# Order of the last routing steps and of the first expert chunks' loads in a gated cross-attention and mixture-of-experts kernel

## The chip, the core and the metric

The kernel runs on one core of one Trainium2 chip. The metric is the device time of one execution in microseconds (us). Runs of the kernel before took 369.24 to 371.98 us, with a median of 370.11 us over three runs.

## The reference

Cut to what matters:

```python
x = x + tanh(g_x) * attention(layernorm(x), ctx, ctx)       # 16 heads of 64, causal
def ffn(x):                                                  # 8 experts, 128 -> 512 -> 128
    e = argmax(softmax(x @ Wr + br))                         # one expert for each token
    out = 0
    for i in range(8):
        xi = x * (e == i)                                    # zero row for other tokens
        out = out + relu(xi @ W1[i] + b1[i]) @ W2[i] + b2[i]
    return out
x = x + tanh(g_f) * ffn(layernorm(x))                        # x: 8 x 256 x 128
```

There are 2048 tokens. A token whose expert is not i still gets `relu(b1[i]) @ W2[i] + b2[i]` from expert i. The kernel adds those constants up beforehand, so that every token is worked on by its own expert alone.

## The kernel before

**Attention.** The eight sequences are taken in four pairs, and each pair in eight steps of two heads: 32 steps, numbered g. A step makes queries, keys, values, scores, exponentials, transposed probabilities and products. A pair's output, its second layer norm and its routing run beside the next pair's steps. The last pair has no next one, so its rest is written out by hand in `last_turns` and `last_routing`. There it is split into two halves, one for each sequence: `a` and `b`, both of class `Half`.

**A half.** `residual` and `out(c)` add the residual and the eight head pairs' share of the output projection into the PSUM tile `y`. `attend` makes the last steps' values in the PSUM tile `o` and evicts them to SBUF, on DVE (L724) or ACT (L726). `statistics` copies `y` to `rows` on ACT (L730), takes the statistics on DVE (L735, L737) and makes the standard deviation on POOL (L739, L740). `turned`, `logits`, `normalized` and `choice` pick each token's expert (`hot`). `apply` writes the normalized rows on ACT (L777). `places` counts on PE (L648 to L652) and on DVE (L653 to L658) at which row of its expert's region of the DRAM array `store` each token goes. `scatter` sends 128 rows there by an indirect DMA from POOL (L673).

**Chunks.** An expert's tokens are worked on in chunks of 128 rows of `store`. There are 23 chunks: `NA` = 5 early ones, which are full before the last pair's tokens come; 8 own ones, one for each expert, whose weights stand ready in SBUF; and 10 later ones, called "rest". Which rows a chunk loads is computed on the device: `plan_full` for the early and own chunks, `plan_rest` for the later ones, 18 short DVE instructions (L846). SyncE (SP) reads a chunk's number (`fetch_number`, L867), asks for its 132 KB of rows (`fetch_rows`, L871) and, for an early or a later chunk, for its expert's 578 KB of weights from the DRAM copy `later` (`fetch_weights`, L881). All of these go through one SP queue in the order of the code.

**A chunk's work.** `turned_rows` transposes the rows (PE L903) and copies them (DVE L905). `first_layer` is eight matmul records on PE (L912), `hidden` four activations on ACT (L920), `residual_rows` adds the constants (L886, on POOL or DVE), `second_layer` is eight matmul records on PE (L928), `sums` adds up (DVE L939), and `store_out` scatters to the output (POOL L946). `second_layer` writes one of two PSUM buffers named `misc`, which it gets back when the `sums` two chunks before has read it.

**Order.** The whole kernel stands under a manual schedule: every engine works off its instructions in the order of the code. In `last_routing`, the early chunks' layers are interleaved with half `b`'s routing. `experts` then loads and works on the own and the later chunks. The rows of own chunks come from `store`, so SP asks for the first of them only when the scatters of the last half have landed. In the text below, r0 to r4 are the rows and w0 to w4 the weights of the early chunks 0 to 4, and r5 are the rows of the first own chunk.

Of the kernel before, what the change touches and what calls it, by code (L numbers as in the profile page):

```python
# [18 lines left out]
B, S, D = 8, 256, 128  # L19
# [16 lines left out]
NA = 5  # L36
# [12 lines left out]
def tile_gated_xattn_moe(  # L49
# [17 lines left out]
    banks = [ps_s.tile([P, 2, 512], F32, tag=f"sc{b}", name=f"sc_{b}") for b in range(2)]  # L67

    def misc(name):
        return ps_m.tile([P, 512], F32, tag="misc", name=name)  # L70
# [197 lines left out]
    _, first = counted("first", [E], [[N, E]])  # L268
# [265 lines left out]
    def turn(g, i):  # L534

        b, j = i // 2, i % 2
        pr = prob[g, b]
        ps = ps_t.tile([P, 512], F32, tag="pt", name=f"pt_{g}_{i}")
        for n in range(3):
            nc.tensor.transpose(ps[:, n * P : (n + 1) * P], pr[:, j, K0 + n * P : K0 + (n + 1) * P], ident)  # L540
        pt = p5.tile([P, 3 * P], F32, tag="probT", name=f"probT_{g}_{i}")
        nc.vector.tensor_copy(pt, ps[:, 0 : 3 * P])  # L542
        probT[g, i] = pt
        if j == 1:
            prob.pop((g, b))
# [125 lines left out]
    def scatter(n, place=None):  # L671
        p, t = n // 4, n % 4
        ins = nc.gpsimd.indirect_dma_start(  # L673
            out=store,
            out_offset=bass.IndirectOffsetOnAxis(ap=places[p][:, t : t + 1] if place is None else place, axis=0),
            in_=rows[:, n],
            in_offset=None,
            bounds_check=E * N - 1,
            oob_is_err=True,
        )  # L680
        free_order(ins, "store")
        if p == NPAIR - 1:
            tc.declare_no_dep(ins.ins, group="full", reason="full chunks have no row left for the last pair's tokens")


    class Half:
# [41 lines left out]
        def statistics(self):  # L728

            nc.scalar.activation(  # L730
                self.rows[:, :, D : 2 * D], self.y.rearrange("p (t d) -> p t d", d=D), AF.Identity
            )
            st, mv = self.tile("st", 2, 6), self.tile("mv", 2, 2)
            for i in range(2):
                nc.vector.bn_stats(st[:, i], self.y[:, i * D : (i + 1) * D])  # L735
            for i in range(2):
                nc.vector.bn_aggr(mv[:, i], st[:, i])  # L737
            self.mv, ve, self.dev = mv, self.tile("ve", 2), self.tile("dev", 2)
            nc.gpsimd.tensor_scalar(ve, mv[:, :, 1], EPS, None, ALU.add)  # L739
            nc.gpsimd.tensor_tensor(self.dev, ve, half, ALU.pow)  # L740

# [40 lines left out]
        def places(self, start, end):  # L782
            places[NPAIR - 1, self.h] = places_of(f"last{self.h}", self.hot, self.n, self.sum, self.pos, start, end, 2)

        def scatter(self):
            for i in range(2):
                scatter(4 * (NPAIR - 1) + self.ts[i], places[NPAIR - 1, self.h][:, i : i + 1])
                apart()

# [53 lines left out]

    def plan_rest():

        q = lambda f, *args: f(*args)  # L846
        n = const.tile([P, E], F32, name="n_rest")
        q(nc.vector.tensor_tensor, n, cb[NPAIR], first, ALU.subtract)
        q(nc.vector.scalar_tensor_tensor, n, done, -float(P), n, ALU.mult, ALU.add)
        m = full_chunks(q, "rest", n, ALU.is_gt, NDYN)  # L850
        whose, k, _ = owners(q, "rest", m, NDYN, done)
        q(nc.vector.tensor_scalar, k, k, 1.0, None, ALU.add)
        q(nc.vector.scalar_tensor_tensor, k, whose, float(NT), k, ALU.mult, ALU.add)
        chunk_of["rest"] = const.tile([P, NDYN], I32, name="load_rest")
        q(nc.vector.tensor_copy, chunk_of["rest"], k)

    chunk_of = {}
    chunks = store.rearrange("(c p) r -> c p r", p=P)
# [16 lines left out]
    def fetch_weights(i):  # L875
        if NA <= i < NA + E:
            w = ws[:, i - NA]
        else:
            at = (W_FULL + i if i < NA else (i - NA - E) % NW) * WROW
            w = arena[:, at : at + WROW]  # L880
            nc.sync.dma_start(out=w, in_=later[bass.ds(number[i] // NT, 1)].rearrange("o p r -> (o p) r"))  # L881
        weights[i] = w[:, 0:FF], w[:, FF:WROW]

    def residual_rows(i, engine):
        r, v = loaded[i], weights[i][1]
        engine.tensor_tensor(r[:, D : 2 * D], r[:, D : 2 * D], v[:, AT_C : AT_C + D], ALU.add)  # L886
# [6 lines left out]
    def turned_rows(ids, beside=False):  # L893

        if not beside:
            ps = h_of[ids[0]] = hidden_bank(ids[0])
            ps = ps[:, 1]
        else:
            ps = ps_t.tile([P, 512], F32, tag="pt", name=f"xs_{ids[0]}")
        n = len(ids)  # L900
        t = p2.tile([P, 512], F32, tag="kT", name=f"xsT_{ids[0]}")
        for k, i in enumerate(ids):
            nc.tensor.transpose(ps[:, k * P : (k + 1) * P], loaded[i][:, 0:D], ident)  # L903
            xsT[i] = t[:, k * P : (k + 1) * P]
        nc.vector.tensor_copy(t[:, 0 : n * P], ps[:, 0 : n * P])  # L905

    def first_layer(i):
        w, x = weights[i][0], xsT.pop(i)
        if i not in h_of:
            h_of[i] = hidden_bank(i)  # L910
        for c in range(NHC):
            nc.tensor.matmul(  # L912
                h_of[i][:, 0, c * P : (c + 1) * P], lhsT=w[:, c * P : (c + 1) * P], rhs=x, start=True, stop=True
            )

    def hidden(i):
        ps, v = h_of.pop(i), weights[i][1]
        h = hT[i] = p2.tile([P, NHC, P], F32, tag="qT", name=f"h_{i}")
        for c in range(NHC):
            nc.scalar.activation(  # L920
                h[:, c], ps[:, 0, c * P : (c + 1) * P], AF.Relu, bias=v[:, AT_B1 + c : AT_B1 + c + 1]
            )
# [37 lines left out]
        nc.gpsimd.memset(warm[:, 0:1], 0.0)  # L960

    def fetch_full():
        for i in range(NA):
            fetch_number(i)
            fetch_rows(i)
        for i in range(NA):
            fetch_weights(i)

    def last_turns():


        g, l = NG - 2, NG - 1
        a = Half(0, misc("y_last0")[:, 0:S], misc("o_last0")[:, 0:S], banks[1][:, 0])
        b = Half(1, banks[0][:, 1, 0:S], banks[0][:, 0, 0:S], banks[1][:, 1])
        steps = plan_full()

        def plan(n):
            for _ in range(min(n, len(steps))):
                f, *args = steps.pop(0)
                f(*args)  # L980

        scatter(8)
        normalized(l, 0)
        turn(g, 0)
        turn(g, 1)
        exps(l, 1)
        scatter(9)
        normalized(l, 1)
        for n in (10, 11):
            scatter(n)  # L990
            apart()
        a.residual()
        a.out(*range(NC - 3))
        plan(4)
        turn(l, 0)
        turn(l, 1)
        a.attend(g, nc.scalar)
        plan(5)
        a.out(NC - 3)
        turn(g, 2)  # L1000
        turn(g, 3)
        a.attend(l, nc.scalar)
        plan(len(steps))
        fetch_full()
        a.out(NC - 2)
        b.residual()
        b.out(0)
        a.out(NC - 1)
        a.statistics()
        turn(l, 2)  # L1010
        turn(l, 3)
        a.turned()
        b.out(1, 2)
        a.logits()
        b.attend(g, nc.vector)
        a.normalized()
        a.choice()
        b.out(3)
        b.attend(l, nc.scalar)
        a.apply()  # L1020
        a.places(cb[NPAIR - 2], cb[NPAIR - 1])
        a.scatter()
        b.out(4, 5, 6, 7)
        return a, b

    def last_routing(a, b):


        e = range(NA)
        b.statistics()  # L1030
        turned_rows(e[:2], True)
        b.turned()
        turned_rows(e[2:], True)
        b.logits()
        b.normalized()
        b.choice()
        first_layer(e[0])
        b.apply()
        hidden(e[0])
        b.places(cb[NPAIR - 1], cb[NPAIR])  # L1040
        first_layer(e[1])
        hidden(e[1])
        second_layer(e[0])
        for i in e[:2]:
            residual_rows(i, nc.gpsimd)
        nc.gpsimd.tensor_copy(early_ids, rows[:, 0:NA, 2 * D : 2 * D + 1].rearrange("p i o -> p (i o)").bitcast(I32))
        b.scatter()
        for i in e[2:]:
            residual_rows(i, nc.gpsimd)
        sums(e[0])  # L1050
        first_layer(e[2])
        hidden(e[2])
        second_layer(e[1])
        sums(e[1])
        plan_rest()
        for i in e[3:]:
            first_layer(i)
            hidden(i)
            second_layer(i - 1)
            sums(i - 1)  # L1060
        second_layer(e[-1])
        sums(e[-1])

    def experts():
        own, more = range(NA, NA + E), range(NA + E, NCH)
# [212 lines left out]
```

## Time and profile before

| what | us |
|---|---|
| median of three runs | 370.11 |
| lowest, highest | 369.24, 371.98 |
| the profiled execution | 369.71 |
| its span, first to last instruction | 367.9 |
| PE busy in the span | 344.5 (94%) |
| DVE, POOL, ACT busy | 240.9, 214.4, 207.5 |
| mean granted TensorE clock | 0.984 |

The profile shows one execution on one core. A row of the timeline gives the start, the busy time, the engine, the source line, the operation with its tiles, and in brackets the idle time just before it with what ended it. The chain of waits starts from the last instruction and goes back, at each step to what released it. A window's row gives its length, the busy time of each engine and the granted clock of TensorE (PEclk, 1.00 is full speed). PE stands for matmuls, PEld for their weight loads, SPq for SyncE's queue of DMA issues. A matmul's end is modelled, so neighbouring records overlap.

### The profile page before, as it was taken

How to read it: one execution, taken by the hardware profiler on the slowest of the kernel's cores; microseconds unless marked ns; L12 is line 12 of the kernel's file. 1: busy time of each engine (PE TensorE's matmuls, PEld its weight loads, DVE VectorE, ACT ScalarE, POOL GpSimd, SP SyncE). 2: the span in 40 equal slices, each digit the busy share in tenths (PEclk: the TensorE clock that was granted, in tenths of full speed). 3: DMA queues.
4: the chain of work that ended last, by engine and by line, in shares of the span. 5: the costliest groups of instructions: out<-in, count | busy, mean ns of one | idle time of the engine just before them, and what ended most of it. 6: DMA issues, size and time to landing. Idle time of an engine off the chain costs nothing.

```text
span 367.9 us, 7926 instructions
## 1 busy us (share of the span) xinstructions
PE 344.5 (94%) x2598; PEld 247.7 (67%) x2598; DVE 240.9 (65%) x838; ACT 207.5 (56%) x743; POOL 214.4 (58%) x306
## 2 busy tenths in 40 slices
PE   8979999999999999999999899999999895979993
PEld 3335666567677776667776566677666774969993
DVE  3637777675667677886766877846788885254441
ACT  2466687755555758555575485555666513436551
POOL 4136665671555577769773388683666663407673
PEclk9899999999999999999999999999999999699999
DMA  6999777766599992000000000075000016679910
GB/s 202 288 164 186 111 114 118 191 240 181 181 385 384 385 384 108 2 2 2 3 0 16 15 16 16 2 321 211 16 16 18 15 61 205 238 215 344 407 50 13
DMA packets 36319, 53.57 MB, mean 146 GB/s; under 512 B 3801, under 2 KB 22829, under 8 KB 36280
## 3 DMA queue, kind: packets, MB, share of 16 engines
q1 hardware_dynamic: 28280, 44.07, 35.0%
q0 software_dynamic: 7360, 8.73, 12.4%
q8 instruction: 20, 0.33, 0.4%
q10 hardware_dynamic: 640, 0.29, 0.3%
q14 instruction: 19, 0.16, 0.1%
HBM read 27.82 MB, written 25.71 MB: 146 GB/s over the span
## 4 chain that ended last, share of the span: by engine, by line
PE 71%; DVE 9%; ACT 9%; DMA 4%; issue 3%; POOL 1%; POOLq 0%; SPq 0%; DVEq 0%; ACTq 0%
PE sc L478 11%; PE o L553 10%; PE pt L540 9%; PE q L438 7%; ACT prob L509 6%; PE y L592 6%; PE k L445 6%; PE v L456 5%; PE hs L912 4%; PE ys L928 4%; DMA arena<-later 3%; DVE sc L488 3%; PE sc L467 2%; ACT kT L447 2%; PE y_last L710 1%
## 5 line engine op out<-in xcount | busy, mean ns | idle before, releaser
L509 ACT ACTIVATE prob<-sc,nmax 128x129 f32<-128x129 f32 (+1 forms) x256 | 105.1, 425 | 92.3 <-DVE nmax L488 92.3
L532 POOL TENSOR_TENSOR prob<-prob,rs 128x256 f32<-128x256 f32 (+1 forms) x128 | 102.6, 858 | 64.8 <-DVE rs L523 64.7
L540 PEld LDWEIGHTS pt<-ident,prob 128*128 128x128 f32 x384 | 46.8, 141 | 52.8 <-issue 47.5
L542 DVE COPY probT<-pt 128x384 f32<-128x384 f32 x128 | 67.1, 544 | 14.8 <-PE pt L540 14.7
L540 PE MATMUL pt<-ident,prob 128*128 128x128 f32 x384 | 63.8, 278 | 1.7 <-DVE probT L542 1.7
L488 DVE CUSTOM_DVE_ANT_0 sc<-sc,bias 128x256 f32<-128x256 f32 x128 | 55.3, 432 | 4.4
L509 ACT ACTIVATION_READ_ACCUMULATOR prob<-sc,nmax 128x1 f32 x256 | 53.5, 209 | 0.0
L478 PE MATMUL sc<-kT,qT 64*128 64x128 f32 (+1 forms) x512 | 50.6, 337 | 0.0
L553 PE MATMUL o<-probT,v 128*64 128x256 f32 x480 | 45.6, 332 | 0.0
L553 PEld LDWEIGHTS o<-probT,v 128*64 128x64 f32 x480 | 29.7, 136 | 18.3 <-issue 8.0
L478 PEld LDWEIGHTS sc<-kT,qT 64*128 64x128 f32 x512 | 36.3, 187 | 4.9
L486 DVE TENSOR_REDUCE nmax<-sc 128x2 f32<-128x258 f32 x64 | 27.0, 421 | 14.7 <-PE sc L478 14.5
L438 PE MATMUL q<-xT,arena 128*128 128x512 f32 x64 | 34.0, 613 | 1.5 <-DVE xT L410 0.8
L445 PE MATMUL k<-cT,arena 128*128 128x512 f32 x64 | 34.4, 620 | 0.8 <-DVE total L336 0.8
L456 PE MATMUL v<-arena,cT 128*128 128x512 f32 x64 | 33.1, 600 | 1.5 <-ACT qT L440 1.5
L440 ACT ACTIVATE qT<-q,bqT 128x512 f32<-128x512 f32 x32 | 22.0, 688 | 13.2 <-PE q L438 12.5
L523 DVE RECIPROCAL rs<-ssum 128x4 f32<-128x4 f32 x64 | 11.0, 173 | 27.7 <-ACT prob L509 22.9
L946 POOL DMA_INDIRECT out_dram<-o,rows x18 | 17.9, 992 | 18.9 <-DVE o L939 15.1
L920 ACT ACTIVATE h<-hs,arena 128x128 f32<-128x128 f32 x60 | 17.1, 367 | 14.3 <-ACT h L920 8.9
L447 ACT ACTIVATE kT<-k,bT 128x512 f32<-128x512 f32 x32 | 22.2, 693 | 3.7 <-PE k L445 3.7
L569 DVE TENSOR_SCALAR arena<-o,bT 128x512 f32<-128x512 f32 x30 | 22.4, 746 | 1.2 <-PE o L553 1.2
L592 PE MATMUL y<-wo_sb,arena 128*128 128x128 f32 x192 | 23.1, 275 | 0.0
(243 smaller groups left out, 505.0 us busy)
## 6 DMA issues: line engine op xcount, KB each, us to landing
store<-blank SPq DMA_DIRECT2D x16, 1056.0 KB, 14.7
arena<-later SPq DMA_DIRECT2D x15, 578.0 KB
rows<-in_ctx_dram POOLq DMA_DIRECT2D x5, 1024.0 KB, 9.1
later<-ws SPq DMA_DIRECT2D x1, 4624.0 KB
rows<-store SPq DMA_DIRECT2D x23, 132.0 KB, 3.7
ws<-in_L_ffn_W_dram SPq DMA_DIRECT2D x1, 2048.0 KB
ws<-in_L_ffn_W_dram SPq DMA_DIRECT2D x8, 256.0 KB, 6.6
x<-in_x_dram SPq DMA_DIRECT2D x4, 256.0 KB
```

The costliest lines, as they stand in the source:

```text
L438: nc.tensor.matmul(ps, lhsT=wq_sb[:, c * P : (c + 1) * P], rhs=xT[p], start=True, stop=True)
L445: nc.tensor.matmul(ps, lhsT=wk_sb[:, c * P : (c + 1) * P], rhs=cT[p], start=True, stop=True)
L447: nc.scalar.activation(kT[g], ps, AF.Identity, bias=bT[:, NC + c : NC + c + 1])
L456: nc.tensor.matmul(ps, lhsT=cT[p][:, t * P : (t + 1) * P], rhs=wv_sb[:, c * P : c * P + 512], start=True, stop=True)
L478: nc.tensor.matmul(s[:, j, at : at + n], lhsT=q[r, b * S + t * P : b * S + (t + 1) * P], rhs=k[r, b * S : b * S + n], start=(t == 1), stop ...
L488: nc.vector.tensor_tensor_reduce(out=s[:, j, K1:U1], in0=s[:, j, K1:U1], in1=bias[:, 2 * (g // NC) + b, K1:U1], scale=-1.0, scalar=-NEG_AL ...
L509: nc.scalar.activation(pr[:, j, lo:hi], s[:, j, lo:hi], AF.Exp, bias=m[:, t, j : j + 1], scale=-1.0 if t else 1.0, accum_out=sm[:, t, j : ...
L532: nc.gpsimd.tensor_tensor(pr[:, :, lo:hi], pr[:, :, lo:hi], r, ALU.mult)
L540: nc.tensor.transpose(ps[:, n * P : (n + 1) * P], pr[:, j, K0 + n * P : K0 + (n + 1) * P], ident)
L542: nc.vector.tensor_copy(pt, ps[:, 0 : 3 * P])
L553: nc.tensor.matmul(o[DK * j : DK * (j + 1), n * P : S], lhsT=v[:, 2 * b + n, cols], rhs=probT[g, 2 * b + j][:, 0:S] if n == 0 else probT[g ...
L592: nc.tensor.matmul(ps[:, i * D : (i + 1) * D], lhsT=attT[p * NC + c][:, t * P : (t + 1) * P], rhs=wo_sb[:, c], start=(c == 0), stop=(c == ...
```

## The change

- `fetch_full` asks for the early chunks' weights between their rows. The order at SP was r0, r1, r2, r3, r4, w0, w1, w2, w3, w4; it becomes r0, r1, w0, r2, r3, w1, r4, w2, w3, w4.
- In `last_turns`, `a.o` moves from a `misc` buffer to the first half of `banks[0]`, `b.o` from the first to the second half of `banks[0]`, and `b.y` from that second half to a `misc` buffer. Four of `b.out`'s last eight matmuls come ahead of `a.places`; `a`'s second scatter moves into `last_routing`.
- `statistics` is cut in two: `deviation` holds its two POOL instructions. For `b`, `deviation` stands ahead of `a`'s second scatter.
- In `last_routing`, `b.turned`, `b.logits` and the first layer and the hidden activations of chunk 0 come ahead of the transposes of chunks 2 to 4. `b.apply` follows chunk 0's activations. The first layer of chunk 1 comes ahead of `b.places`, its activations follow. `b`'s scatters come ahead of the copy of `early_ids`.
- `plan_rest` gives back its 18 instructions as a list. They are issued five at a time between the sums of the early chunks, where they were all issued after the sums of chunk 1.

```diff
@@ class Half
-            self.mv, ve, self.dev = mv, self.tile("ve", 2), self.tile("dev", 2)
+            self.mv = mv
+
+        def deviation(self):
+            mv, ve, self.dev = self.mv, self.tile("ve", 2), self.tile("dev", 2)
             nc.gpsimd.tensor_scalar(ve, mv[:, :, 1], EPS, None, ALU.add)
             nc.gpsimd.tensor_tensor(self.dev, ve, half, ALU.pow)
...
-        def scatter(self):
-            for i in range(2):
+        def scatter(self, *which):
+            for i in which:
@@ def plan_rest
-        q = lambda f, *args: f(*args)
+        steps = []
+        q = lambda *step: steps.append(step)
...
+        return steps
@@ def fetch_full
+        weights_behind = {1: (0,), 3: (1,), 4: (2, 3, 4)}
         for i in range(NA):
             fetch_number(i)
             fetch_rows(i)
-        for i in range(NA):
-            fetch_weights(i)
+            for k in weights_behind.get(i, ()):
+                fetch_weights(k)
@@ def last_turns
-        a = Half(0, misc("y_last0")[:, 0:S], misc("o_last0")[:, 0:S], banks[1][:, 0])
-        b = Half(1, banks[0][:, 1, 0:S], banks[0][:, 0, 0:S], banks[1][:, 1])
+        a = Half(0, misc("y_last0")[:, 0:S], banks[0][:, 0, 0:S], banks[1][:, 0])
+        b = Half(1, misc("y_last1")[:, 0:S], banks[0][:, 1, 0:S], banks[1][:, 1])
...
         a.statistics()
+        a.deviation()
...
         a.apply()
+        b.out(4, 5)
         a.places(cb[NPAIR - 2], cb[NPAIR - 1])
-        a.scatter()
-        b.out(4, 5, 6, 7)
+        a.scatter(0)
+        b.out(6, 7)
@@ def last_routing
         e = range(NA)
+        steps = []
+        plan = lambda n: [f(*args) for f, *args in [steps.pop(0) for _ in range(min(n, len(steps)))]]
         b.statistics()
+        b.deviation()
+        a.scatter(1)
         turned_rows(e[:2], True)
         b.turned()
-        turned_rows(e[2:], True)
         b.logits()
         b.normalized()
         b.choice()
         first_layer(e[0])
+        hidden(e[0])
+        turned_rows(e[2:], True)
         b.apply()
-        hidden(e[0])
+        first_layer(e[1])
         b.places(cb[NPAIR - 1], cb[NPAIR])
-        first_layer(e[1])
         hidden(e[1])
         second_layer(e[0])
         for i in e[:2]:
             residual_rows(i, nc.gpsimd)
+        b.scatter(0, 1)
         nc.gpsimd.tensor_copy(early_ids, rows[:, 0:NA, 2 * D : 2 * D + 1].rearrange("p i o -> p (i o)").bitcast(I32))
-        b.scatter()
         for i in e[2:]:
             residual_rows(i, nc.gpsimd)
+        steps += plan_rest()
         sums(e[0])
-        first_layer(e[2])
-        hidden(e[2])
-        second_layer(e[1])
-        sums(e[1])
-        plan_rest()
-        for i in e[3:]:
+        for i in e[2:]:
             first_layer(i)
             hidden(i)
+            plan(5)
             second_layer(i - 1)
             sums(i - 1)
+        plan(5)
         second_layer(e[-1])
         sums(e[-1])
+        plan(len(steps))
```

## The prediction

> **What bounds the kernel now.** I read the page first (PE busy 94% of the span), then the chain of waits over the end, then the timeline of the stretch in which the chain leaves PE, then windows for the clock.
>
> ```profile
> PE 344.5 (94%) x2598; PEld 247.7 (67%) x2598; DVE 240.9 (65%) x838; ACT 207.5 (56%) x743; POOL 214.4 (58%) x306
> 306.82 2.12 DMA rows<-store
> 309.95 10.07 DMA arena<-later
> 320.10 0.35 DVE o L939
> 320.45 0.12 DVE n_rest L846
> ...
> 324.32 0.06 DVE load_rest L846
> 324.44 0.36 DVE o L939
> ```
>
> The number ahead of each piece of the chain is its start. PE holds the chain until 305 and again from 326.77. Between, it passes through a load of rows, 10 us of weights and 4 us of the plan's DVE instructions. The timeline of that stretch has the steps that I shall move:
>
> ```profile
> 303.17 0.71 PE L710 MATMUL sc<-wo_sb,arena 128*128 128x128 f32 x4 [0.59 <-DVE arena L724]
> 305.26 2.05 PE L710 MATMUL sc<-wo_sb,arena 128*128 128x128 f32 x16 [0.32 <-ACT arena L726]
> 312.22 2.05 PE L912 MATMUL hs<-xsT,arena 128*128 128x128 f32 x8 [2.56 <-DMA arena<-later]
> 317.42 0.98 POOL L673 DMA_INDIRECT store<-rows,posi_last  x1 [0.18 <-ACT h L920]
> 321.01 6.02 SPq L871 DMA_DIRECT2D rows<-store  x9
> 324.94 1.13 PE L928 MATMUL ys<-arena,h 128*128 128x128 f32 x8 [1.37 <-DVE o L939]
> 326.77 1.16 PE L912 MATMUL hs<-xsT,ws 128*128 128x128 f32 x8 [0.59 <-DVE xsT L905]
> ```
>
> The reader sees PE wait 2.56 us for w0, the last half's second scatter at 317.42, r5 asked for only at 321.01 (the SP waits name that scatter, 5.6 us), a PE wait behind the plan, and the first own chunk's first layer at 326.77. From there PE is busy 34.52 of 35.60 us, one chunk each 1.89 us, to the end at 367.9. So the time is **326.77 plus a fixed 41.1 us of span, plus 1.8 us around it** (369.71 against 367.9). What moves the start of that layer moves the end. My sum stands against 369.71, which lies 0.4 below the median of 370.11, inside the runs' spread.
>
> ```profile
> 7.70:11.10 3.40, 1.97 (x10) 1.15 (x10) 1.86 (x5) 1.65 (x4) 1.66 (x9) 1.00 0.75 207
> 11.10:14.50 3.40, 3.40 (x4) 1.39 (x5) 3.40 (x15) 0.69 (x1) 0.00 (x0) 0.50 1.10 346
> 284.20:287.60 3.40, 1.95 (x31) 1.53 (x29) 3.13 (x11) 2.85 (x14) 1.37 (x2) 1.00 0.00 0
> 308.10:311.50 3.40, 1.01 (x9) 0.69 (x6) 2.46 (x13) 1.26 (x3) 1.86 (x4) 1.00 0.97 307
> 311.50:318.30 6.80, 6.08 (x32) 6.04 (x33) 1.14 (x7) 2.28 (x8) 3.13 (x6) 0.50 0.92 354
> ```
>
> In these windows the second figure is PE's busy time and the last but two the granted clock. After 1.01 us of PE work in 3.40, the clock is at half for 6.8 us: eight matmul records take 2.05 us there instead of 1.06.
>
> **The change, part by part.**
>
> *PSUM tiles.* `b.out(3)` at 303.17 reads a head pair that was long in SBUF, yet waits for the DVE eviction of `b.o`, and `b.out(4)` at 305.26 for the ACT one: `b.y` and `b.o` are halves of one tile, `banks[0]`. With `b.y` in `misc` both waits go. `b.out(3)` (0.45) runs under the DVE eviction, `b.attend` starts at 303.17 instead of 303.81, `b.out(4, 5)` (0.89) fills the wait for `hot`, `a.places` takes 0.3, `b.out(6, 7)` 0.89: `b.y` is done at about 306.1 instead of 307.3. `a.places` is some 0.4 later by it, and `a`'s first scatter starts at 307.0 instead of 306.58; nobody waits for that one alone. `a.o` in `banks[0]` costs nothing: the exponentials that read it ended at 291.9, its first matmul was at 294.69.
>
> *`deviation` ahead of `a`'s second scatter.* On POOL the first scatter (1.08, memset 0.12) ends at 308.1 and the statistics are there by 307.4, so `dev` comes at 309.2, where it was 310.04; the choice follows in 1.6 (310.08 to 311.68), so `hot` is there at 310.85. Queued behind `dev` is `a`'s second scatter, 307.96 before, 309.4 now. In this stretch a scatter has taken up to 7.4 us to land (the rows' tile view: 2.1/3.3/7.4), so 316.8 at worst, still ahead of `b`'s.
>
> *Loads on SP.* A weight issue takes 0.58 to 0.65 of SP, a number with its rows 1.17. r0 and r1 stay at 301.44 and 303.18; w0 goes out at 303.83 (307.47 before), r2 and r3 at 305.1 and 306.3, w1 at 306.9 (308.04), **r4 at 308.1 (306.82)**, then w2 to w4 at 308.7 to 309.9, as before. w0 landed 4.65 after its issue (307.47 to 312.12), w1 and the others some 2.0 apart (314.0 ... 320.0). So w0 lands near 308.0 (3.3 to 4.65 after its issue: 307.1 to 308.5), and w4 near 317.3, since one of five loads of 2 us each is out of the way early, or 320.0 if the cadence doesn't hold. r4 is what this part costs. Alone, rows land 2.1 after their issue; now 578 KB stand ahead. The trace has one queue serving r4 and then w0, w1 ... in order. The Trainium skill, "DMA: Bandwidth & Descriptors" (Queues, rings and completion order), speaks against the change here: each DMA engine consumes a ring in ring order, so small rows can't pass large weights. By the 2.1 us of the rows alone r4 would land at 310.2; by the rule it lands behind w1, 306.9 + 3.3 to 4.65, plus 0.6 of its own: 310.8 to 312.2. I take 311.4, since the cadence of 2.0 is nearer to the short end and `a`'s scatter shares the engines.
>
> *Order on PE.* Logits end at about 308.0; the first layer of chunk 0 (0.89 at full clock) runs 308.0 to 308.9, against 312.22 to 314.24. Then the transposes of chunks 2 to 4 wait for r4: 311.4 to 311.75, and behind them stand chunk 1's first layer (to 312.7) and `b.places` (to 313.0; before 314.3). `hot` (310.85) is no longer what is late; r4 is. ACT has chunk 0's activations (1.14) and then `b.apply` (0.88) done by 311.1, ahead of any use.
>
> *The scatter and r5.* From the end of `b.places` to the first scatter it was 1.7 (314.3 to 316.02), to the second 1.4 more, from there to SP's release 3.4 (320.82), to the issue 0.2, to landing 2.1, to the first layer of chunk 5 about 0.8 (transpose, copy). From 313.0 that gives 314.7, 316.1, 319.5, 319.7, 321.8, **322.6**. Behind the scatters stand `early_ids` (0.2) and the residuals of chunks 2 to 4 (0.45 each) on POOL: chunk 2's sum waits for its own until about 317.9, and its buffer is wanted by chunk 4's second layer at 319.5.
>
> *The plan in steps.* 18 instructions took 320.37 to 324.49, 0.23 each. Five are 1.15, with a sum 1.5, beside 1.79 of PE for two layers: hidden. The PE wait of 1.37 and the late copy of chunk 5 go. Were r5 in no better time than before (asked at 321.01, landed 323.1), this part alone would be worth 1.5. Chunk 4's layers follow w4: 317.3, first layer 318.3, activations 1.14, second layer to 320.4, so PE is free before r5 lands.
>
> **Sum.** 326.77 - 322.6 = 4.2 earlier: 369.71 - 4.2 = **365.5 us**. The bounds: r4 at 310.8 and a scatter that lands in 2.4 (317.42 to 319.8, if the last straggler is another DMA's doing) give 321.0, held by PE to about 321.2: 364.1. r4 at 312.2 gives 323.4: 366.3.
>
> **Rivals.**
>
> *The clock drops all the same (0.27).* PE now idles from 308.9 to 311.4, 2.5 us, much as the 2.56 before, but between two first layers. The skill, "TensorE: Matmul & The Clock Gate" (Why this matters for your kernels), asks for gaps under some 3 us; by it neither gap should have cost a thing. The windows above say otherwise: 1.01 us of work in 3.40 was followed by half clock, and so was 1.97 at 7.70, nearly all transposes, while 1.95 of mixed work at 284.20 was not. So the kind of work counts beside the gap, and the new window has 0.7 to 1.3 us, with matmuls in it. By the rule 365.5. By the row, six groups of eight at half clock add 1.0 each, partly under the weights' arrival: the second layer of chunk 4 ends at 323.8, chunk 5 starts at 324.6: **367.5**. I take full clock, since the quiet window before had only transposes and logits.
>
> *Rows behind weights (0.06, the other side).* Chunks 2 to 4's transposes stand ahead of chunk 1 and of `b.places` on PE. If the engines mix r4 with w1 to w4 instead of serving them in order, r4 lands with the last, near 317.5, and everything from `b.places` on moves 6.1: 328.7, **371.6**. It decides once r4 lands after 315.6. For it: `a`'s scatter took 7.4 us in this traffic. Against: w0 and w1 landed one by one.
>
> *Given back later (0.05).* The later chunks' weights become the end: **369.7**. The last of them was issued at 345.89, needs some 3.4, and is used at 326.77 + 17 x 1.89 = 358.9: 9.6 us of room against 4.2 taken. So it is unlikely.
>
> **Chances.** Forecast 0.62, the rivals as given. Both of the first are below 369.7, so 363.9 to 368.4 holds eight in ten. A change of 1%, about what a measurement of this kernel tells from none, is 366.4: the forecast's case lies below it nine times in ten, the half-clock case seldom. Faster 0.60, within 1% 0.36, slower 0.04.
>
> **What would show it.** Right: L710 of `b.out` without a wait for L724 or L726; a first layer at about 308.0; PE's wait for rows until 311 to 312 at L903; the second scatter near 316; no wait of L928 for L939; chunk 5's first layer at 322 to 323. Wrong: a granted clock of 0.50 after 311; r4 landing past 313; chunks at the end further apart than 1.89.

## The result and the profile after

The kernel after took **367.36 us** (median of ten runs, 365.03 to 369.84) against 370.24 us for the kernel before beside it: a ratio of 0.9916, with a 95% interval from 0.9892 to 0.994. It is 2.9 us faster. A second set on another chip of the same speed gave 367.52 against 370.31, 0.9926 (0.9902 to 0.995). The forecast was 365.5, the case with half clock 367.5.

The profiled execution took 366.26 us, with a span of 364.6. Its lines have moved: the transposes of an early chunk are now L908 (L903), the first layers L917 (L912), the second layers L933 (L928), the sums L944 (L939), the rows' loads L876 (L871) and the plan L1039 (L846). First PE's row of the page, then the chain of waits over the changed stretch (start, length, what):

```profile
PE 343.1 (94%) x2598; PEld 246.7 (68%) x2598; DVE 241.8 (66%) x838; ACT 207.5 (57%) x743; POOL 214.4 (59%) x306
```

```profile
308.26 4.38 DMA rows<-store
312.63 0.05 issue
312.68 0.48 PE xs L908
313.15 1.71 PE hs L917 x8
```

The 10 us of weights and the 4 us of the plan have left the chain. In their place stands one load of rows, r4: issued at 308.26, used at 312.68, 4.4 us where the same load took 2.1 before. The timeline of the steps that were shown of before:

```profile
302.85 0.71 PE L710 MATMUL y_last<-wo_sb,arena 128*128 128x128 f32 x4
304.31 1.16 PE L710 MATMUL y_last<-wo_sb,arena 128*128 128x128 f32 x8
308.43 1.14 PE L917 MATMUL hs<-xsT,arena 128*128 128x128 f32 x8
312.68 0.48 PE L908 MATMUL xs<-ident,rows 128*128 128x128 f32 x1 [2.89 <-DMA rows<-store]
312.95 1.92 PE L917 MATMUL hs<-xsT,arena 128*128 128x128 f32 x8
317.90 0.97 POOL L673 DMA_INDIRECT store<-rows,posi_last  x1 [0.19 <-ACT h L925]
320.54 4.71 SPq L876 DMA_DIRECT2D rows<-store  x8
320.74 1.95 PE L933 MATMUL ys<-arena,h 128*128 128x128 f32 x16
323.49 1.16 PE L917 MATMUL hs<-xsT,ws 128*128 128x128 f32 x8 [0.38 <-DVE xsT L910]
```

`b.out` no longer waits for an eviction, chunk 0's first layer runs at 308.43 without a wait for w0, and L933 has no wait for a sum. PE now waits 2.89 us for r4, and the next first layer takes 1.92. The windows tell why (second figure PE's busy time, last but two the granted clock):

```profile
309.00:312.40 3.40, 0.78 (x8) 0.55 (x6) 1.40 (x9) 1.90 (x6) 2.40 (x5) 1.00 0.96 300
312.40:315.80 3.40, 3.12 (x18) 3.06 (x19) 1.24 (x6) 0.90 (x4) 0.05 (x1) 0.50 0.99 377
323.50:359.00 35.50, 34.53 (x305) 34.10 (x305) 14.82 (x53) 20.53 (x72) 22.25 (x27) 1.00 0.72 255
```

The wait was followed by half clock for one window of 3.4 us. The last row is the stage of own and later chunks: as full as before.

For all profiles below I use one measure: **the lead**, from the first half's first statistics (the first L735 on DVE of the last half `a`) to the first layer of the first own chunk. It is 326.77 - 300.08 = 26.7 us before and 323.49 - 300.42 = 23.1 after. What follows it lasted 41.1 us in both, so all of the gain arose in the lead.

The ten timed runs of after, by the mean TensorE clock granted in each:

| granted clock | times, us |
|---|---|
| 0.998 | 365.03 |
| 0.987 to 0.991 | 365.67, 366.13, 366.26 |
| 0.978 to 0.982 | 367.24, 367.48, 367.69, 367.90, 368.15, 369.84 |

One window at half clock lowers the mean by about 0.005 (1.7 of 365 us). The forecast of 365.5 lies between the run at 0.998 and the three in the second row; by this the other six had lost three or four windows, somewhere in the whole span. Within the last row the times still differ by 2.6 us, so the clock is not all that differs between runs.

### The profile page after: what moved, and what is told of

It is laid out like the page before. It is cut to its first block, busy times and chain, and to the rows that moved or that the text cites. A ratio compares the mean times of both kernels' runs of the same rounds, so it can differ in the third digit from the quotient of the medians.

```text
span 364.6 us, 7926 instructions
## 1 busy us (share of the span) xinstructions
PE 343.1 (94%) x2598; PEld 246.7 (68%) x2598; DVE 241.8 (66%) x838; ACT 207.5 (57%) x743; POOL 214.4 (59%) x306
## 4 chain that ended last, share of the span: by engine, by line
PE 70%; ACT 8%; DVE 8%; DMA 5%; issue 4%; POOL 3%; POOLq 0%; SPq 0%; DVEq 0%; ACTq 0%
PE sc L478 10%; PE pt L540 9%; PE o L553 9%; PE q L438 6%; PE y L592 6%; ACT prob L509 6%; PE hs L917 6%; PE k L445 5%; PE ys L933 5%; PE v L456 5%; DVE sc L488 3%; DMA rows<-in_ctx_dram 2%; PE y_last L710 2%; PE sc L467 2%; ACT kT L447 2%
## 5 line engine op out<-in xcount | busy, mean ns | idle before, releaser
L478 PE MATMUL sc<-kT,qT 64*128 64x128 f32 (+1 forms) x512 | 51.6, 342 | 0.0
L445 PE MATMUL k<-cT,arena 128*128 128x512 f32 x64 | 33.5, 605 | 0.8 <-DVE total L336 0.8
L440 ACT ACTIVATE qT<-q,bqT 128x512 f32<-128x512 f32 x32 | 22.0, 687 | 13.9 <-PE q L438 13.1
L523 DVE RECIPROCAL rs<-ssum 128x4 f32<-128x4 f32 x64 | 11.0, 173 | 27.1 <-ACT prob L509 22.3
L592 PE MATMUL y<-wo_sb,arena 128*128 128x128 f32 x192 | 23.1, 275 | 0.0
```

The costliest lines, as they stand in the source:

```text
L445: nc.tensor.matmul(ps, lhsT=wk_sb[:, c * P : (c + 1) * P], rhs=cT[p], start=True, stop=True)
L478: nc.tensor.matmul(s[:, j, at : at + n], lhsT=q[r, b * S + t * P : b * S + (t + 1) * P], rhs=k[r, b * S : b * S + n], start=(t == 1), stop ...
L592: nc.tensor.matmul(ps[:, i * D : (i + 1) * D], lhsT=attT[p * NC + c][:, t * P : (t + 1) * P], rhs=wo_sb[:, c], start=(c == 0), stop=(c == ...
```

## The experiments

Four of the kernels (plan in steps alone, loads alone, after with old loads, after with places first) shared a chip on which the kernel before took 376.51 us. Their profiles have 46.9 to 49.7 us behind the lead instead of 41.1; what held that stage there stays open. Their ratios are against the kernel before on that chip. The last column counts the windows of 3.4 us in the lead that had half clock; before has two of them and a lead of 26.7, the first profile of after has one and 23.1.

| kernel | us | before beside it | ratio, 95% interval | lead, us | half-clock windows in it |
|---|---|---|---|---|---|
| after, again | 367.52 | 370.31 | 0.9926 (0.9902, 0.995) | 24.0 | 2 |
| plan in steps alone | 375.76 | 376.51 | 0.997 (0.9948, 0.9993) | 24.0 | 1 |
| after, plan in a block | 368.55 | 370.14 | 0.9955 (0.9928, 0.9981) | 25.9 | 2 |
| loads alone | 378.51 | 376.51 | 1.0041 (1.0017, 1.0065) | 26.6 | 2 |
| after, old loads | 378.85 | 376.51 | 1.005 (1.0028, 1.0072) | 26.7 | 3 |
| after, matmuls added | 365.31 | 370.31 | 0.987 (0.9844, 0.9895) | 23.4 | 1 |
| before, matmuls added | 367.89 | 370.14 | 0.9944 (0.9921, 0.9967) | 25.6 | 0 |
| after, old tiles | 365.06 | 370.31 | 0.9874 (0.9838, 0.9911) | 22.1 | 0 |
| old tiles, matmuls added | 366.19 | 370.14 | 0.9901 (0.9871, 0.993) | 22.3 | 0 |
| after, places first | 375.18 | 376.51 | 0.9933 (0.9891, 0.9976) | 24.1 | 2 |
| after, r4 ahead of w1 | 366.66 | 370.14 | 0.99 (0.987, 0.993) | 23.7 | 2 |
| both of these | 365.90 | 370.31 | 0.9883 (0.9858, 0.9909) | 23.8 | 1 |

What was expected of the first row:

> The kernel after, unchanged, timed again beside the others of this set, as their measure. Theory and rival alike: 0.8% below before; first own chunk's first layer some 23 us after the first half's statistics, against 26.7 before.

It came out as 367.52 us, with a lead of 24.0 in its profile.

A lead is one profile's, so two leads can be compared only where the same number of half-clock windows fell into them. In the kernel after, with or without the old tiles and the added matmuls, it was 22.1 and 22.3 us without such a window, 23.1 and 23.4 with one, and 24.0 with two: about 1 us for each.

### The plan: alone, and taken back

```diff
 # before, with this alone
+        steps += plan_rest()
         sums(e[0])
...
-        plan_rest()
+            plan(5)                      # between the sums, as in after
 # after, with this alone taken back
-            plan(5)
...
-        plan(5)
+            plan(len(steps) if i == e[2] else 0)   # all behind chunk 1's sum
```

> The kernel before, with the 18 plan instructions issued in steps between the sums and nothing else. Theory (three separate gains: the plan's block 1.4, the loads and the order of PE the rest, cut by r4's late landing and a short half clock): 1.4 to 1.5 us off, about 368.8, the first own chunk's first layer some 1.4 earlier, with r5 landing as before. Rival (the plan is the whole gain, the rest washes out): 2.9 off, about 367.4.

> The kernel after, with all 18 plan instructions in one block behind the sums of chunk 1, as before. Theory (the plan is in the way of PE's second layers only where it is a block): PE waits about 1 to 1.5 us for a misc buffer at L933 again, first own chunk 0.5 to 1.5 us later than after (r5 hides a part): 368 to 369. Rival (r5 sets the start, so the block is hidden): same as after, 367.4.

Alone, the steps bring 0.3%: 1.1 us by the ratio, 0.75 between the medians. Taken back they cost 1.0 us (368.55 against 367.52), with intervals that overlap. The kernel with the block has the wait again, in its timeline:

```profile
323.61 1.13 PE L933 MATMUL ys<-arena,h 128*128 128x128 f32 x8 [1.59 <-DVE o L944]
```

Its lead is 25.9, against 24.0 for after's second profile, which has the same two half-clock windows (from 310.6 and 310.7). So r5 does not hide the block, and the second rival falls. The lead of 24.0 with the plan in steps alone looks like the whole gain, but that profile has one half-clock window (313.4 to 316.8) where before's has two, and its run took 373.29 us against a median of 375.76. By the times the lower end of the interval for the steps alone is 0.9948, above the 0.992 of the whole change, so the first rival falls too. The plan is worth about 1 us of the 2.9 by the times, and up to 1.9 by the two leads with the same clock.

### The loads: alone, and taken back

```diff
 # before, with this alone (after, with this taken back: the other way round)
+        weights_behind = {1: (0,), 3: (1,), 4: (2, 3, 4)}
         for i in range(NA):
             fetch_number(i)
             fetch_rows(i)
-        for i in range(NA):
-            fetch_weights(i)
+            for k in weights_behind.get(i, ()):
+                fetch_weights(k)
```

> The kernel before, with w0 and w1 asked for between the rows and nothing else. Theory: r4 lands near 312.6, and in the old order of PE the transposes of chunks 2 to 4 stand ahead of the last half's logits, so logits, choice and places come 1 to 3.5 late: no gain, 369.5 to 371.5. Rival (early weights are the gain by themselves): first layer of chunk 0 moves ahead by 3 us, about 368.

> The kernel after, with the old order of loads (all rows, then all weights). Theory: w0 lands at about 312, and now the transposes, chunk 1's first layer and b.places all stand behind chunk 0's first layer, so places come at about 316, the scatter at 318 and 319.5, first own chunk at about 326: 2 us slower than after, about 369.4. Rival (the order of loads hardly matters, the plan and the tiles carry the gain): 367 to 368.

The new loads alone are slower than before by 0.4%, and all the rest of the change without them by 0.5%. Their leads (26.6 and 26.7) are no shorter than before's. With the new loads in the old order of PE, the logits stand behind r4; with the old loads in the new order, everything stands behind w0. Two lines of the first kernel's timeline, then two of the second's:

```profile
312.53 0.47 PE L903 MATMUL xs<-ident,rows 128*128 128x128 f32 x1 [1.75 <-DMA rows<-store]
312.80 0.86 PE L751 MATMUL sc<-wrc,xt_last 128*128 128x8 f32 x4
```

```profile
311.82 2.05 PE L917 MATMUL hs<-xsT,arena 128*128 128x128 f32 x8 [3.86 <-DMA arena<-later]
313.65 0.85 PE L908 MATMUL xs<-ident,rows 128*128 128x128 f32 x3
```

The logits (L751) were at 309.16 in before. The second kernel came out slower than I expected; behind its wait of 3.86 us the profile has 10 us of half clock. The loads and the order of PE are one move: neither gained without the other. Together, with the new tiles and the plan still in a block, they are the kernel of the section above, at 0.9955.

### The clock: matmuls that no result uses

```diff
 # after
         first_layer(e[0])
         hidden(e[0])
+        keep_awake(6)                    # six bf16 matmuls on constants
         turned_rows(e[2:], True)
 # before
         b.choice()
+        keep_awake(10)
         first_layer(e[0])
```

> The kernel after, with six matmuls of 128x512 bf16 on constants put on PE behind chunk 0's first layer, where PE otherwise waits 2.9 us for r4 (work added, no result uses it). Theory (the half clock behind that wait costs about 1 us: chunk 1's first layer took 1.9 instead of 1.06): no clock of 0.50 in this stretch, chunk 1's first layer 1.06, first own chunk about 1 us earlier than after. Rival (r4 and the scatter set the start, the clock does not matter): same as after.

> The kernel before, with ten matmuls of 128x512 bf16 on constants put on PE between the last half's logits and chunk 0's first layer, where PE waits 2.56 us for w0. Theory (the half clock costs before as much as after or more): first layers of chunks 0 and 1 at 1.06 instead of 2.05, the plan's block some 2 us earlier, first own chunk 2 to 3 us earlier: about 367.5, as after without any of its moves. Rival (the weights' landing paces the early chunks in before, so the clock is hidden): within 0.5 of before, 370.

Six added matmuls made the kernel after **2.2 us faster**, 365.31 against 367.52 on the same chip, with intervals apart; four of the six runs took 365.3. Ten made the kernel before 2.25 us faster, about three quarters of what the whole change brought. So by the times the clock matters in both. Before's profile with them has no half clock anywhere in the lead, with no other change of order:

```profile
307.10:310.50 3.40, 2.80 (x16) 1.73 (x18) 2.51 (x13) 0.91 (x3) 2.03 (x5) 1.00 0.96 285
310.50:313.90 3.40, 1.82 (x17) 1.26 (x14) 1.25 (x8) 1.50 (x5) 0.45 (x1) 1.00 0.98 349
```

I had expected the first own chunk 2 to 3 us earlier there, and the lead came out only 1.1 shorter (25.6). Chunk 1's first layer then waits 1.98 us for w1, and the plan's block makes PE wait 1.51 us (1.37 in before): the rival, that the weights' landing paces the early chunks, holds for a part. Another 0.65 us between the two profiles lies ahead of the lead, where before's has a half-clock window (11.1 to 14.5) and this one none. Matmuls added at 309 cannot have caused that.

Not all runs were saved. The profile of after with six has chunk 1's first layer at 1.06 as expected, but PE still waits 1.67 us for r4 behind them, and the next windows are:

```profile
311.80:315.20 3.40, 1.73 (x18) 1.48 (x18) 0.73 (x2) 0.73 (x3) 0.81 (x2) 1.00 0.97 346
315.20:318.60 3.40, 3.40 (x19) 3.40 (x18) 2.07 (x11) 1.10 (x4) 1.55 (x3) 0.50 0.65 259
```

That run took 367.69 us. I had expected no half clock in the stretch and a lead about 1 us below after's 23.1; 23.4 came out. There is no profile of a run at 365.3; that those four ran at a fuller clock is read from their means, 0.990 to 0.997, against 0.981 to 0.990 for the runs of after on that chip.

### The PSUM tiles of before

```diff
-        a = Half(0, misc("y_last0")[:, 0:S], banks[0][:, 0, 0:S], banks[1][:, 0])
-        b = Half(1, misc("y_last1")[:, 0:S], banks[0][:, 1, 0:S], banks[1][:, 1])
+        a = Half(0, misc("y_last0")[:, 0:S], misc("o_last0")[:, 0:S], banks[1][:, 0])
+        b = Half(1, banks[0][:, 1, 0:S], banks[0][:, 0, 0:S], banks[1][:, 1])
```

> The kernel after, with the PSUM tiles of before (b.y beside b.o in banks[0]). Theory (r4 is what is late, so the 1.1 us that the tiles save ahead of it are hidden): b.out waits for the evictions again, b.y is done 0.7 to 1.1 later, yet the first own chunk starts within 0.3 us of after: same as after. Rival (the tiles carry a part of the gain): about 0.7 to 1.1 us slower than after.

> The kernel after with the PSUM tiles of before, and the six constant matmuls behind chunk 0's first layer. Theory (old tiles won because chunk 0's first layer ran later and PE's idle time before r4 was 1.9 instead of 2.9 us): with the idle time nearly filled no run falls to half clock, 364.5 in all runs, first own chunk about 22.1 us after the first half's statistics. Rival (old tiles won by something else than the clock): the added matmuls change nothing against the old tiles alone, 365.1 with single runs at 368.

I expected no change and got 365.06 us. `b.out` waits again and chunk 0's first layer starts 1.3 us later (9.3 after the statistics instead of 8.0). Lines of the timeline on PE and SP, then the window:

```profile
308.44 1.14 PE L917 MATMUL hs<-xsT,arena 128*128 128x128 f32 x8
309.42 0.38 PE L908 MATMUL xs<-ident,rows 128*128 128x128 f32 x2
311.36 0.33 PE L908 MATMUL xs<-ident,rows 128*128 128x128 f32 x1 [1.56 <-DMA rows<-store]
311.52 1.06 PE L917 MATMUL hs<-xsT,arena 128*128 128x128 f32 x8
...
315.62 0.97 POOL L673 DMA_INDIRECT store<-rows,posi_last  x1 [0.19 <-ACT h L925]
318.26 4.06 SPq L876 DMA_DIRECT2D rows<-store  x7
320.57 0.30 PE L908 MATMUL hs<-ident,rows 128*128 128x128 f32 x1 [0.44 <-DMA rows<-store]
```

```profile
309.45:312.86 3.41, 1.85 (x21) 1.60 (x19) 2.09 (x11) 2.14 (x7) 2.00 (x4) 1.00 0.94 362
```

r4 came at the same place (12.2 after the statistics, 12.3 in after), so the idle time ahead of it is 1.56 instead of 2.89 us. Chunk 1's first layer takes 1.06, and the lead is 22.1, ended by r5 (the 0.44), the end that the prediction had for after. In these profiles the step of the change that makes `b.y` earlier only lengthens PE's wait for r4. By the medians (365.06 against 367.52) that step is a loss of 2.5 us, but the two intervals overlap (one ends at 0.9911, the other starts at 0.9902), so the loss is likely and not shown. Adding the six matmuls to the old tiles gave no more: full clock and 22.3 in the lead of the profile, but 366.19 in the median, with half of the runs near 365.5 and half near 367. That was a miss for both expectations. The mean clock of the slower three was 0.992 to 0.993, that of the others 0.993 to 0.997, so it accounts for a part at most. What else slowed those runs is not settled.

### Three other orders

```diff
 # places first
         hidden(e[0])
-        turned_rows(e[2:], True)
         b.apply()
-        first_layer(e[1])
         b.places(cb[NPAIR - 1], cb[NPAIR])
+        turned_rows(e[2:], True)
+        first_layer(e[1])
         hidden(e[1])
 # r4 ahead of w1
-        weights_behind = {1: (0,), 3: (1,), 4: (2, 3, 4)}
+        weights_behind = {1: (0,), 4: (1, 2, 3, 4)}
```

> The kernel after, with b.places ahead of the transposes of chunks 2 to 4 and of chunk 1's first layer, loads as in after. Theory (what is late in after is b.places behind r4): places at about 311.1, the scatters at 312.8 and 314.2, r5 asked for some 2 us earlier; the first own chunk then waits for PE's early chunks instead: about 1 us faster than after, 366.4. Rival (the early chunks' layers at half clock set the end anyway): no change, 367.4.

> The kernel after, with w1 asked for behind r4 instead of ahead of it, and nothing else. Theory (a wait for r4 behind w1 leaves PE idle for 2.9 us, and that idle time brings the half clock): r4 lands 1 to 1.5 us earlier, PE's longest idle time falls under 2 us, chunk 1's first layer runs at full clock in most runs and the time is near 365.3, as with the added matmuls. Rival (w1 lands late instead, the idle time is only moved): 367.4 as after.

> The kernel after, with w1 asked for behind r4 instead of ahead of it, and b.places ahead of the transposes of chunks 2 to 4. Theory (r4 stands behind w1 in the ring, and b.places behind r4): r4 lands near 310 instead of 312.7, the wait for it is under 1 us, the scatters start near 312.8 and 314.2, first own chunk 1 to 1.5 us earlier than after: 0.3% faster than after. Rival (w1 then lands late and chunk 1's first layer takes r4's place, with the same idle time and the same half clock): same as after.

With places first, the second scatter went out 3.7 us earlier, counted from the statistics (13.9 instead of 17.6 in after's second profile), yet the lead is 24.1 against 24.0. Both profiles have two half-clock windows, and PE's early chunks end then: the rival holds. Issued ahead of w1, r4 came 9.9 us after the statistics instead of 12.3, but chunk 1's first layer then waited for w1:

```profile
310.57 0.33 PE L908 MATMUL xs<-ident,rows 128*128 128x128 f32 x1 [0.56 <-DMA rows<-store]
312.22 2.05 PE L917 MATMUL hs<-xsT,arena 128*128 128x128 f32 x8 [1.32 <-DMA arena<-later]
```

It ran at half clock and the time is within the noise of after: the idle time was only moved. The two together are 1.6 us below after in their set, the intervals overlapping (0.9909 and 0.9902), so that gain is likely and not shown. It did not come from the scatter. Timelines of POOL and SP of that kernel:

```profile
313.30 0.97 POOL L673 DMA_INDIRECT store<-rows,posi_last  x1 [0.19 <-issue]
319.90 0.95 SPq L876 DMA_DIRECT2D rows<-store  x2
```

This scatter, sent into the stream of weights, held SP for 6.6 us, and the last weights landed only then (PE waits for them until 319.57). After's, sent when the stream was over, held SP for 2.6 (317.90 to 320.54): the DMA traffic there had fallen from 320 to 111 GB/s at 316.5.

## Why the prediction was right and where it was wrong

The direction, the places and the range were right. The likeliest case was the wrong one of two: **the step that failed is "I take full clock"**.

- *Tiles, deviation, w0.* Set against the first statistics (0.34 later in after's profile), `b.y` came at 306.2 (forecast 306.1), `hot` at 310.7 (310.85), chunk 0's first layer at 308.1 (308.0). These steps held, the 1.3 us that the tiles save among them. What I had not priced is that an earlier start ahead of a fixed arrival makes the idle time longer.
- *r4.* Forecast 311.4, bounds 310.8 to 312.2; it came at 312.3, 0.9 late and just past the bound. That rows queue behind w1 was right, and the kernel with r4 first shows it (2.3 us earlier). That they can't pass was my conclusion: the page cited for it, "DMA: Bandwidth & Descriptors" of the Trainium skill (Queues, rings and completion order), gives the order in which descriptors are consumed, and says that a later one may finish its write before an earlier one.
- *The clock.* I set the row (1.01 us of work in 3.40, then half clock) against the rule of the Trainium skill, "TensorE: Matmul & The Clock Gate" (Why this matters for your kernels), which asks for no gaps over some 3 us, and took the rule's value, because the new window would hold matmuls of a first layer. It held them (0.56 of its 0.78 us), and half clock followed the wait of 2.89 all the same: the row was right. The added matmuls, which took away a part of the half clock, gained 2.2 us in the median. The half-clock case was priced at 367.5; 367.4 and 367.5 came out. That it fits so closely is in part luck: it had two windows and a slow scatter, where after's profile has one window, a later r4 and a faster scatter. The chances of 0.62 and 0.27 were the wrong way round.
- *Scatter and r5.* I had 3.6 us from the second scatter's start to r5's issue; 2.6 came out, since the weights were gone by then. This gave back 1.0, so the profile's lead is 23.1 against a forecast of 22.5, in spite of one half window and a late r4.
- *The plan.* Forecast 1.5 by itself; about 1 by the times of the two kernels that isolate it, 1.9 by the two leads with the same clock.
- *Later chunks.* 41.1 us behind the lead, as forecast. Rows behind weights on the other side did not happen: r4 came well before w4.

## What to carry to other kernels

When work is pulled forward to an arrival that is fixed, ask how long TensorE then sits idle, not only what no longer waits: here the earlier step seems to have cost more than it saved, and ten matmuls that nobody reads brought the kernel before three quarters of what the whole reordering did. Loads and the order of the instructions that use them are to be moved together, since here each without the other was slower. Before two profiles are compared, their half-clock windows are to be counted. And a forecast that turns on the granted clock should take the value of the nearest row of its own trace.

## What the runs showed of the hardware

The half clock did not need a gap of 3 us: waits of 2.56 and 2.89 us were followed by it. The low stretch of 3.4 us that held 0.78 to 1.73 us of PE work was followed by half clock in the rows above. With 1.82 to 1.85 it stayed full in two kernels (before with ten matmuls, after with old tiles), while after's second profile fell after 1.82 (with two windows at half) and the kernel with r4 first after 2.14 (its two waits there were 0.56 and 1.32 us):

```profile
307.20:310.60 3.40, 1.82 (x14) 1.58 (x14) 1.72 (x11) 1.70 (x7) 3.10 (x7) 1.00 0.98 309
310.60:317.40 6.80, 5.15 (x28) 5.09 (x29) 2.09 (x10) 1.51 (x5) 1.65 (x4) 0.50 0.74 276
```

Those were the windows of after's second profile; these are of the kernel with r4 first:

```profile
308.20:311.60 3.40, 2.14 (x15) 1.71 (x15) 1.80 (x11) 1.77 (x6) 2.94 (x7) 1.00 0.85 301
311.60:318.40 6.80, 6.18 (x32) 6.15 (x33) 2.21 (x12) 1.59 (x7) 2.65 (x6) 0.50 0.84 294
```

So somewhere about 2 us of 3.4 the outcome is open, and what else decides it stays open.

In before's profile the clock changes at 11.12, 14.53, 311.50 and 318.32 us, which lie 1, 87 and 2 times 3.413 us apart: a grid of 3.41 us. It lies elsewhere against the program in each profile. Counted from the first statistics, a change fell at 11.97 in the first profile of after and at 10.72 in the second. The wait for r4 lay almost whole within one window of the grid in the first, which was followed by one window at half clock, and across two in the second, which had two. That may be one reason why one kernel's runs spread over 4 us.

One of the plan's steps (`wide_rest`, 80 elements) took 1.21 us in after's profile, beside POOL's copy and three adds, and 0.24 in after's second profile. It cost nothing there; the cause wasn't tried.
